# Graph attention and nucleus diffusion: rank constants formed at the start, and half of a block of S products moved from ahead of the first attention into it

## The chip, the cores and the metric

The kernel runs on one core of a Trainium2 chip. A core has five engines that work side by side, each through its own queue in order: TensorE (PE in the profile; PEld is its weight load), VectorE (DVE), ScalarE (ACT), GpSimd (POOL) and SyncE (SP, which issues most of the loads and stores). The metric is the time of one execution in microseconds on the device. Before the change the median of four runs is 3581.87 us (3580.59 to 3583.27).

## The reference

There are 2708 nodes with 512 features, in two layers; each adds its result to its input, `x = x + f(relu(layernorm(x)))`.

Layer 0 is graph attention with 8 heads over an adjacency matrix `adj` of zeros and ones. Layer 1, cut to what matters here:

```python
S = adj + eye(n)
Rf = S / row sums of S              # forward, rows scaled
Rb = S / column sums of S           # as written, scaled over its rows
Xf, Xb, Xa = X, X, X
for s in range(2):
    logits = (Xa @ W1) @ W2 @ (Xa @ W3).T
    A = softmax over the nucleus of each row   # largest entries up to 0.9 of the mass
    Xf = Rf @ Xf;  Xb = Rb @ Xb;  Xa = A @ Xa
    Z = Z + Xf @ U1[s] + Xb @ U2[s] + Xa @ U3[s]
out = layernorm(X + Z) * gamma + beta
```

Ties at the edge of the nucleus are broken by the index of the column; the kernel needs ranks of equal keys for that in its second step.

## The kernel before

All of it is in one function. The nodes are cut into 22 tiles of 128 rows (`NT`; the last has 20), the tiles into 11 `pairs`, and every two pairs into a `quad` of four tiles (`quads`).

**Layer 0** (lines 203 to 460) is put in order by a scheduler from the dependences of its instructions. It begins with LayerNorm, one tile at a time (`moments` and `cleared`, from lines 133 and 219 on): VectorE's statistics, POOL's power, VectorE's `h`, POOL's maximum with zero, then PE's transposes (L268) and products (L277, L280), and VectorE's `fw` (L298). Its pool of large tiles (`fw`, `b_b`, `beta_b` and others) is freed at the end. Its last tiles are normed at about 1060 us, and VectorE's first and last splits of `v` follow at 1070 and 1081 us.

**Constants.** Behind layer 0 stand the small constants of layer 1, and with them those for the ranks, lines 498 to 506: `ones` filled with 1, `across` its running sum along the row, `down` the same number down the partitions (by way of the identity matrix), and `below_d`, which is 1 where `across < down`. `ones` and `across` lie in a pool `ramps` of their own, which is freed at once.

**Layer 1** takes two steps, `s` = 0 and 1 in the code. Step 1 of the title is the first, `s = 0`, where `last` is false; the change is in it alone. PE, ACT, DVE and SP run in the order in which the code is written (`manual_schedule`); POOL is put in order by the scheduler. For each pair there is a `Logits` object `lg[i]`:

- `queries()` loads its `q_t` (L525, on SP). `products()` forms its two rows of logits (L538 on PE) and copies them into two tiles `p` (L540 on ACT). There are four `p` tiles, so pair i takes those of pair i - 2. Its products go through the tiles `t`, two in PSUM, which the transposes of the attention use too.
- `maxima` (L565, DVE) and `exp()` (L575 to L597): two exponentials over each row on ACT, some points on POOL, and then for all pairs but the first twelve passes on ACT that the code calls looks (L572 with `nth`), and POOL's sums of them.
- `search()` on VectorE finds the threshold of the nucleus: rounds that measure the mass above a point (L651), into which `early()` puts the maxima of the pair after the next, then `late()`, and then `finish()` (L845, L847, L780), which writes the kept rows into two tiles `keep` and ends in a branch (L929) for the rare rows with ties; `rden` (L940) is the first instruction behind it.
- `attended()` turns the rows of `keep` (L1098 on PE, L1102 on ACT) and multiplies them by the values `va` (L1120), in 12 steps of up to four tiles of columns; `mixed()` then multiplies by `U3` (L1160, two batches) and projects the new keys (L161).

Beside this run the products with `S`, quad by quad, each in two parts. `part(half, b)` returns a list of small steps, and `paced(steps, n)` runs the first n of them and takes them off the list. In the first step of the diffusion, for even b, it is 22 steps `product(c)`: each loads `hl` (512 KB) and `s_r` (256 KB) over SP (L1003, L1005) and does eight matmuls (L1013) into four tiles `q`. For odd b it is 11 steps: `across` (L1020, four ACT copies and stores `tt_d`), four `through` with U1 (eight matmul records each, L1030, with a load `u_k` on SP), `scaled` (L1040, four ACT copies `xe`), four `through` with U2, and `scaled`. The first `scaled` of an odd part has its rows split at once by VectorE (`split_rows`, L182 and L183) and stored by POOL (L184, to `fhl_d`); those of the second wait in `pending`.

Ahead of the first attention the code runs parts 0 and 1 and then, while VectorE searches for the first pair, all of part 2:

```python
                    others = part(half, 2)
                    paced(others, len(others))
                done = []
                ...
                for g in range(-1, NP):
                    fills = []
                    if last or g >= 0:
                        others = part(half, g + 2 if last else g + 3)
                    if 0 <= g < NP - 2:
                        lg[g + 2].products()
```

So the loop at g = 0 takes the third pair's products, then the attention of the first pair with part 3 as `others`: one step of them behind each of the 12 steps of `attended`, two at the start of `mixed` and one at each of its eight products. At the same time VectorE searches for the second pair. g = 1 takes the fourth pair's products, the attention of the second pair and part 4, and so on.

Of the kernel before, what the change touches and what calls it, by code (L numbers as in the profile page):

```python
# [9 lines left out]
F32 = mybir.dt.float32  # L10
BF16 = mybir.dt.bfloat16
# [4 lines left out]
OP = mybir.AluOpType  # L16
# [8 lines left out]
P = 128  # L25
# [28 lines left out]
def kernel(  # L54
# [19 lines left out]
    nc = tc.nc  # L74
# [6 lines left out]
    NT = -(-N // P)  # L81
# [14 lines left out]
    const = ctx.enter_context(tc.tile_pool(name="const", bufs=1))  # L96
# [21 lines left out]

    ident = const.tile([P, P], F32, name="ident")
    make_identity(nc, ident)  # L120
    nhalf = const.tile([P, 1], F32, name="nhalf")
    nc.vector.memset(nhalf, -0.5)

# [79 lines left out]
    with ExitStack() as l0:  # L203
# [13 lines left out]
        with tc.tile_pool(name="l0w", bufs=1) as wp, tc.tile_pool(name="l0p", bufs=2) as pp, \  # L217
# [44 lines left out]
            for t in range(NT):  # L262
# [8 lines left out]
                for k in range(KD):  # L271
                    nc.scalar.activation(h_t[:, k, :pr], pt[:, k, :pr], AF.Copy,
                                         accum_out=hs[:, k, t:t + 1])
# [138 lines left out]
        for ci, tiles in enumerate(tchunks):  # L412
# [4 lines left out]
            for t in range(NT):  # L417
# [5 lines left out]
                if pr < P or cw < wide:  # L423
                    nc.gpsimd.memset(s_c.bitcast(F32), 0.0)
                nc.scalar.activation(s_c[:pr, :cw], a_c[t][:pr, :cw], AF.Copy,  # L425
                                     accum_out=cpart[:pr, t, ci:ci + 1])
# [67 lines left out]
    for i in range(G + 1):  # L494
        nc.vector.memset(weights[:, i:i + 1], float(1 << i))
    NA = len(ABOUT)

    down = const.tile([P, 1], F32, name="down")
    below_d = const.tile([P, P], BF16, name="below_d")
    with tc.tile_pool(name="ramps", bufs=1) as pool:  # L500
        ones = pool.tile([P, P], F32, name="ones")
        across = pool.tile([P, P], F32, name="across")
        nc.vector.memset(ones, 1.0)
        nc.vector.tensor_tensor_scan(across, ones, ones, 0.0, OP.add, OP.bypass)
        nc.vector.scalar_tensor_tensor(ones, across, 1.0, ident, op0=OP.mult, op1=OP.mult, accum_out=down)
        nc.vector.tensor_scalar(below_d, across, down, None, op0=OP.is_lt)

    class Logits:

# [440 lines left out]
    for s in range(STEPS):  # L950
        last = s == STEPS - 1
        with ExitStack() as st:
# [129 lines left out]
            def paced(steps, n):  # L1082
                for step in steps[:n]:
                    step()
                del steps[:n]
# [151 lines left out]
            with tc.manual_schedule(engines={PE, ACT, DVE, SP}):  # L1237
                junk = wide.tile([P, -(-N // 4) * 2], F32, name="junk", bufs=1)
                lg = [Logits(pools, s, grp, keys, rank) for grp in pairs[:2]]
                half = []  # L1240
                others = part(half, 0)
                if last:
                    lg[0].queries()
                    lg[0].products()
                    for load in values(nc.gpsimd):
                        load()
                    heads, counts = ranked(junk.bitcast(BF16)[:, :N], list(range(early_tiles, NT)), "keep", 2)
                    steps = lg[0].exp(looks=False)
                    paced(heads, len(heads))
                    for step in lg[0].maxima + steps + counts:  # L1250
                        step()
                    lg[1].queries()
                    paced(others, NT // 2)
                    spread()
                    lg[1].products()
                    paced(others, len(others))
                else:
                    paced(others, 3)
                    for n, (t, v) in enumerate(unasked):
                        asked(s, slice(n * early_tiles // len(unasked) * P, (n + 1) * early_tiles // len(unasked) * P))  # L1260
                        paced(others, 1)
                        split_rows(parts, nc.vector, v[:rows[t]], t, vhl_d)
                        v_t = transposed(up, ps_t, v, rows[t], "v_t")
                        project(small, ps_t.tile([P, 512], F32, name="t"), v_t, t, s)
                    asked(s, slice(early_tiles * P, N), nc.gpsimd)
                    lg[0].queries()
                    lg[1].queries()
                    ahead = [c for c in chunks if c[1] <= early_tiles * P]
                    lg[0].products(ahead)
                    paced(others, 3)  # L1270
                    lg[0].products(chunks[len(ahead):])
                    steps = lg[0].exp(looks=False)
                    for step in lg[0].maxima + steps:
                        step()
                    paced(others, 9)
                    lg[1].products()
                    paced(others, len(others))
                    others = part(half, 1)
                    loads = values(nc.sync)
                    while others:  # L1280
                        paced(others, 1)
                        paced(loads, 2)
                    others = part(half, 2)
                    paced(others, len(others))
                done = []
                ready = None
                left = []
                for g in range(-1, NP):

                    fills = []  # L1290

                    if last or g >= 0:
                        others = part(half, g + 2 if last else g + 3)
                    if 0 <= g < NP - 2:
                        lg[g + 2].products()
                    if g < 0:
                        paced(left, len(left))
                    if g + 3 < NP:
                        lg.append(Logits(pools, s, pairs[g + 3], keys, rank))
                        lg[g + 3].queries()  # L1300
                    norms = [normed(t, y) for t, y in done] if last else []
                    done = []

                    if g == NP - 1 and not last:
                        asked(s + 1, slice(0, early_tiles * P))
                        heads, counts = ranked(junk.bitcast(BF16)[:, :N], list(range(early_tiles)), "p", 4)
                        fills += heads + [lambda: paced(counts, len(counts))]
                    if g >= 0:
                        final = g == NP - 1 and not last
                        att = attended(pairs[g], *ready, fills, others, 1 if final else 3 if g or not last else len(tgroups) + 1)  # L1310
                    def early(g=g):
                        if g + 2 < NP:
                            fills.extend(lg[g + 2].exp())
                        first, *more = lg[g + 2].maxima if g + 2 < NP else [lambda: None]

                        def begin():
                            if g >= 0:
                                paced(pending, len(pending))
                            first()

                        return begin, lambda: [x() for x in more], lambda: [rest() for rest in norms]

                    def late(g=g):
                        if g >= 0:
                            out_ = rest_of(att)
                            if last:
                                done.extend(zip(pairs[g], out_))
                            else:
                                mixed(pairs[g], out_, others, fills, final)
                            keeps = min(len(others), len(quads[g // 2 + 1])) if last and others else 0  # L1330
                            while len(others) > keeps or fills:
                                paced(others, min(2, len(others) - keeps))
                                paced(fills, 1)
                            left.extend(others)
                            others.clear()
                            return


                        paced(fills, len(fills))
                        if last:  # L1340
                            paced(others, len(others))

                    if g + 1 < NP:
                        opened = None
                        if g >= 0:
                            opened = Opened(lg[g + 1], True, junk)
                            opened.bracket()
                        ready = search(lg[g + 1], opened, junk, early, late)
                        if g < 0 and not last:
                            paced(pending, len(pending))  # L1350
                    else:
                        for rest in norms:
                            rest()
                        paced(pending, len(pending))
                        late()
                if last:
                    for rest in [normed(t, y) for t, y in done]:
                        rest()
                    paced(stores, len(stores))
# [31 lines left out]
```

## Time and profile before

| | |
|---|---|
| median of 4 runs | 3581.87 us |
| the profiled execution | 3589.24 us, its span 3587.4 us |
| PE busy | 3329.9 us, 93% |
| DVE busy | 2655.7 us, 74% |
| ACT busy | 1504.2 us, 42% |
| POOL busy | 859.4 us, 24% |
| mean granted PE clock | 0.974 |
| part 2 of S, products L1013 | 1172.0 to 1239.1 us |
| first L1098 of the first attention | 1246.87 us |
| first L1098 of the second attention | 1348.52 us |

In the rows below a line of the timeline begins with its start, its duration, engine, source line and operation, then `out<-in` by the program's names, the shape and how many instructions follow one another; in brackets stands how long the engine was idle before, and what released it. For PE a matmul of four-byte values shows as more than one record. A row of windows has the stretch, its length, the busy time of PE, PEld, DVE, ACT and POOL with their instructions, the granted PE clock as a share of full speed, the mean busy share of the 16 DMA engines, and GB/s.

### The profile page before, as it was taken

How to read it: one execution, taken by the hardware profiler on the slowest of the kernel's cores; microseconds unless marked ns; L12 is line 12 of the kernel's file. 1: busy time of each engine (PE TensorE's matmuls, PEld its weight loads, DVE VectorE, ACT ScalarE, POOL GpSimd, SP SyncE). 2: the span in 40 equal slices, each digit the busy share in tenths (PEclk: the TensorE clock that was granted, in tenths of full speed). 3: DMA queues.
4: the chain of work that ended last, by engine and by line, in shares of the span. 5: the costliest groups of instructions: out<-in, count | busy, mean ns of one | idle time of the engine just before them, and what ended most of it. 6: DMA issues, size and time to landing. Idle time of an engine off the chain costs nothing. (4 is left out here: it accounts for less than half of the span.)

```text
span 3587.4 us, 34134 instructions
## 1 busy us (share of the span) xinstructions
PE 3329.9 (93%) x10797; PEld 1721.2 (48%) x10797; DVE 2655.7 (74%) x4828; ACT 1504.2 (42%) x2269; POOL 859.4 (24%) x1074
## 2 busy tenths in 40 slices
PE   7998999998978799999999999889999999999877
PEld 4433333333445546455464544355555555565433
DVE  4587888889985645463754655598889998889994
ACT  2344211111103666564656672344545564445610
POOL 4114241415321111222121221311112222122211
PEclk9999999999999999999999999999999999999989
DMA  3477424232318726344452622684556545566433
GB/s 115 145 246 247 153 95 138 76 123 85 102 67 292 270 91 208 103 164 162 152 195 90 214 82 69 206 286 144 197 182 232 173 166 183 197 208 205 157 129 119
DMA packets 251348, 579.99 MB, mean 162 GB/s; under 512 B 33945, under 2 KB 67593, under 8 KB 248291
## 3 DMA queue, kind: packets, MB, share of 16 engines
q1 hardware_dynamic: 229063, 503.39, 42.3%
q0 software_dynamic: 22064, 74.09, 5.3%
q8 instruction: 86, 1.41, 0.2%
q14 instruction: 135, 1.11, 0.1%
HBM read 471.68 MB, written 105.68 MB: 161 GB/s over the span
## 5 line engine op out<-in xcount | busy, mean ns | idle before, releaser
L1120 PE MATMUL a<-va,at 128*128 128x512 f32 (+2 forms) x1936 | 889.0, 599 | 7.4 <-ACT at L1102 7.3
L443 PE MATMUL po<-e,fw 128*65 128x512 f32 (+4 forms) x2112 | 838.5, 552 | 33.3 <-DVE e L441 21.0
L441 DVE SCALAR_TENSOR_TENSOR e<-r_b,kk,a_c 128x512 f32<-128x512 f32 (+4 forms) x1056 | 750.4, 739 | 72.2 <-PE po L443 21.8
L572 ACT ACTIVATE junk_a<-p,nth 128x2708 uint8<-128x2708 f32 (+1 forms) x240 | 612.7, 2553 | 57.2 <-POOL nth L587 52.7
L1010 PE MATMUL q<-hl,s_r 128*128 128x512 f32 x1936 | 528.5, 422 | 66.4 <-DMA s_r<-s_d 62.5
L443 PEld LDWEIGHTS po<-e,fw 128*65 128x65 f32 (+1 forms) x2112 | 286.7, 140 | 545.3 <-issue 270.4
L1120 PEld LDWEIGHTS a<-va,at 128*128 128x128 f32 (+2 forms) x1936 | 338.8, 187 | 378.1 <-issue 335.5
L1010 PEld LDWEIGHTS q<-hl,s_r 128*128 128x128 f32 x1936 | 364.6, 192 | 219.1 <-issue 63.1
L651 DVE SCALAR_TENSOR_TENSOR junk<-p,th 128x2708 bf16<-128x2708 f32 (+1 forms) x132 | 424.9, 3219 | 3.2
L1102 ACT COPY at<-t 128x512 f32<-128x512 f32 (+3 forms) x308 | 140.1, 476 | 495.4 <-PE t L1098 491.5
L1013 PE MATMUL q<-s_r,hl 128*128 128x512 f32 (+1 forms) x1056 | 282.9, 415 | 40.4 <-DMA s_r<-s_d 37.5
L1030 PE MATMUL q<-u_k,v 128*128 128x512 f32 x704 | 317.0, 593 | 0.8 <-ACT v L1020 0.8
L540 ACT COPY p<-t 128x452 f32<-128x452 f32 (+2 forms) x264 | 129.9, 537 | 341.0 <-PE t L538 268.4
L1013 PEld LDWEIGHTS q<-s_r,hl 128*128 128x128 f32 x1056 | 193.2, 195 | 124.1 <-issue 49.6
L565 DVE TENSOR_REDUCE nmx<-p 128x1 f32<-128x2708 f32 (+1 forms) x44 | 130.5, 2968 | 110.3 <-ACT p L540 110.3
L1030 PEld LDWEIGHTS q<-u_k,v 128*128 128x128 f32 x704 | 133.6, 190 | 150.5 <-issue 145.0
L847 DVE MAX8 vn<-keep 128x8 f32<-128x2708 f32 (+1 forms) x66 | 196.8, 2982 | 2.3
L425 ACT ACTIVATE s_c<-a_c 128x512 fp32r<-128x512 f32 (+3 forms) x132 | 76.2, 577 | 248.5 <-DMA a_c<-in_adj_t_dram 122.8
L1160 PE MATMUL a<-u_k,v_t 128*128 128x512 f32 (+1 forms) x352 | 170.0, 623 | 1.9 <-DMA u_k<-in_L_gnn_U_dram 1.9
L1098 PEld LDWEIGHTS t<-ident,keep 128*128 128x128 f32 (+1 forms) x968 | 114.9, 140 | 114.2 <-issue 89.4
L538 PE MATMUL t<-keys,q_t 128*128 128x452 f32 x528 | 149.1, 403 | 21.8 <-ACT p L540 21.4
L1098 PE MATMUL t<-ident,keep 128*128 128x128 f32 (+1 forms) x968 | 147.3, 275 | 18.9 <-DVEq L934 11.6
(311 smaller groups left out, 3311.8 us busy)
## 6 DMA issues: line engine op xcount, KB each, us to landing
s_r<-s_d SPq DMA_DIRECT2D x330, 256.0 KB
hl<-vhl_d SPq DMA_DIRECT2D x132, 512.0 KB
hl<-fhl_d SPq DMA_DIRECT2D x132, 512.0 KB
hl<-bhl_d SPq DMA_DIRECT2D x132, 512.0 KB
u_k<-in_L_gnn_U_dram SPq DMA_DIRECT2D x184, 256.0 KB
arow<-in_adj_dram SPq DMA_DIRECT2D x21, 1354.0 KB
s_d<-s_c SPq DMA_DIRECT2D x88, 256.0 KB
a_c<-in_adj_t_dram SPq DMA_DIRECT2D x84, 256.0 KB
```

The source lines that it names most:

```text
L441: nc.vector.scalar_tensor_tensor(e[:pr, :cw], r_b[:pr, i, :cw], kk[:pr, t, hd:hd + 1], a_c[t][:pr, :cw], op0=OP.max, op1=OP.mult)
L443: nc.tensor.matmul(po[i][:, :cw], lhsT=fw[:pr, t, hd, :], rhs=e[:pr, :cw], start=(t == 0), stop=(t == NT - 1))
L538: nc.tensor.matmul(pl[:, :c1 - c0], lhsT=q[:, i], rhs=self.keys[:, c0:c1], start=(i == 0), stop=(i == 1))
L572: nc.scalar.activation(junk[:pr], self.p[i][:pr], func, **kw)
L651: nc.vector.scalar_tensor_tensor(self.junk_b[:pr], p, th, p, op0=OP.is_ge, op1=OP.mult, accum_out=dst)
L847: v.max(vs, keep[0][:pr])
L1010: nc.tensor.matmul(half[j], lhsT=s_r[:, j * P:(j + 1) * P], rhs=hl[:, h], start=(c == 0 and h == 0), stop=(c == NT - 1 and h == 1))
L1013: nc.tensor.matmul(half[j][:, :w], lhsT=hl[:, h, j * P:(j + 1) * P], rhs=s_r[:, :w], start=(c == 0 and h == 0), stop=(c == NT - 1 and h == 1))
L1030: nc.tensor.matmul(half[j], lhsT=across_t[-1][k][:, j * P:(j + 1) * P], rhs=u_k, start=(start and k == 0), stop=(start and k == KD - 1))
L1098: nc.tensor.transpose(pt[:rows[c], j, :pr], keep[i][:pr, cols[c]], ident[:pr, :pr])
L1120: nc.tensor.matmul(pa[:pr], lhsT=at[:rows[c], j, :pr], rhs=va[:rows[c], c, :], start=(c == 0), stop=(c == NT - 1))
L1160: nc.tensor.matmul(pz[i][:rows[t]], lhsT=v_t[i][:, k, :rows[t]], rhs=u_k, start=(k == 0), stop=(k == KD - 1))
```

## The change

It has two edits. The constants for the ranks are formed right behind the identity matrix, ahead of layer 0, and their pool `ramps` is freed before the pool of layer 0 is opened. And of part 2 only 11 of the 22 products run ahead of the first attention (`NT // 2`); the other 11 stay in `others`, and part 3 is put behind them, so that the first attention has 22 steps instead of 11 beside it. Later attentions have no rest to take over. In the last step of the diffusion nothing changes.

```diff
     make_identity(nc, ident)
+    down = const.tile([P, 1], F32, name="down")
+    below_d = const.tile([P, P], BF16, name="below_d")
+    with tc.tile_pool(name="ramps", bufs=1) as pool:
+        ones = pool.tile([P, P], F32, name="ones")
+        across = pool.tile([P, P], F32, name="across")
+        nc.vector.memset(ones, 1.0)
+        nc.vector.tensor_tensor_scan(across, ones, ones, 0.0, OP.add, OP.bypass)
+        nc.vector.scalar_tensor_tensor(ones, across, 1.0, ident, op0=OP.mult, op1=OP.mult, accum_out=down)
+        nc.vector.tensor_scalar(below_d, across, down, None, op0=OP.is_lt)
...
     NA = len(ABOUT)
-
-    down = const.tile([P, 1], F32, name="down")
-    below_d = const.tile([P, P], BF16, name="below_d")
-    with tc.tile_pool(name="ramps", bufs=1) as pool:
...
                         paced(loads, 2)
                     others = part(half, 2)
-                    paced(others, len(others))
+                    paced(others, NT // 2)
...
-                    if last or g >= 0:
-                        others = part(half, g + 2 if last else g + 3)
+                    if last:
+                        others = part(half, g + 2)
+                    elif g >= 0:
+                        others += part(half, g + 3)
```

In the order of the instructions the first edit moves the loads `b_b` and `beta_b` on SP from the head of the queue to between the two loads `v_b`, since `b_b` lies where `ones` and `across` were, and VectorE's and POOL's statistics of some of layer 0's first tiles ahead of a product `fw`. The second moves on PE, ACT, SP and POOL what belongs to the steps named; the order on VectorE in layer 1 stays the same.

More of the change, by code (lines that the diff above doesn't have):

```diff
@@ L496 @@
     NA = len(ABOUT)
-    down = const.tile([P, 1], F32, name="down")
-    below_d = const.tile([P, P], BF16, name="below_d")
-    with tc.tile_pool(name="ramps", bufs=1) as pool:
[L501 to L506, printed above, removed]
     class Logits:
```

## The prediction

> **What bounds the kernel now.** I read the page first: PE is busy for 93% of the span, and from the start of the diffusion step to 2000 us for 97% of it (483.4 of 500 us in the windows from 1500 to 2000). Whatever lengthens PE's chain there lengthens the kernel. Then I read the timeline of each engine around the moved half block. PE:
>
> ```profile
> 1192.75 2.11 PE L1013 MATMUL q<-s_r,hl 128*128 128x512 f32 x8 [0.70 <-DMA s_r<-s_d]
> 1196.93 7.31 PE L1013 MATMUL q<-s_r,hl 128*128 128x512 f32 x24 [2.07 <-DMA s_r<-s_d]
> ...
> 1239.13 0.98 PE L538 MATMUL t<-keys,q_t 128*128 128x452 f32 x4
> ...
> 1246.87 1.09 PE L1098 MATMUL t<-ident,keep 128*128 128x128 f32 x8 [0.20 <-ACT p L540]
> ...
> 1321.72 1.12 PE L148 MATMUL t<-ident,xa 128*128 128x128 f32 x4 [3.09 <-ACT xa L1128]
> 1322.63 9.59 PE L1160 MATMUL a<-u_k,v_t 128*128 128x512 f32 x16
> 1332.05 1.95 PE L161 MATMUL t<-v_t,kw 128*128 128x128 f32 x16
> 1333.83 7.03 PE L1160 MATMUL a<-u_k,v_t 128*128 128x512 f32 x16
> 1340.30 1.39 PE L538 MATMUL t<-keys,q_t 128*128 128x452 f32 x4
> ```
>
> Eight records are one product. Nine end by 1194.8 and three follow from 1196.93, so the eleventh ends near 1201.5. The other eleven last until L538 at 1239.13, with waits for their loads between them: two windows show the cause, a DMA share of 0.95 in the second.
>
> ```profile
> 1172.00:1201.50 29.50, 23.99 (x87) 18.07 (x86) 22.21 (x48) 22.63 (x21) 8.65 (x11) 0.88 0.77 261
> 1201.50:1239.10 37.60, 25.97 (x92) 18.73 (x92) 16.63 (x46) 21.03 (x16) 3.81 (x9) 0.91 0.95 343
> ```
>
> ScalarE and VectorE in the same stretch, and at the end of the first attention:
>
> ```profile
> 1222.57 0.19 ACT L572 ACTIVATION_READ_ACCUMULATOR junk_a<-p,nth 128x1 f32 x1
> 1239.75 0.97 ACT L540 COPY p<-t 128x452 f32<-128x452 f32 x2 [16.99 <-PE t L538]
> ```
>
> ```profile
> 1282.59 0.43 DVE L182 TENSOR_SCALAR split_hl<-xe 128x512 int32<-128x512 int32 x1 [25.59 <-ACT xe L1040]
> 1291.52 3.03 DVE L845 SCALAR_TENSOR_TENSOR keep<-p,th 128x2708 f32<-128x2708 f32 x1
> 1313.32 3.04 DVE L780 SCALAR_TENSOR_TENSOR keep<-p,cut 128x2708 f32<-128x2708 f32 x1 [4.45 <-PE t L1098]
> 1323.55 0.17 DVE L940 RECIPROCAL rden<-den 128x2 f32<-128x2 f32 x1 [3.43 <-DVEq L929]
> ```
>
> Two things stand here. ACT's looks at the second pair end at 1222.76, so ACT is 17 us ahead of PE, not more. And VectorE's `finish()` of the second search stands behind four splits of `xe`, which wait for U1's products on PE. It ends at 1323.55, 16.75 us before PE comes to the fourth pair's L538 at 1340.30. That L538's results go into the `p` tiles of the second pair, which `finish()` reads to its end: the built program lets the first copy L540 into each `p` tile wait for VectorE as well as PE.
>
> **Edit 2, the start of the first attention.** Eleven products go from PE's path ahead of the attention, 1201.5 to 1239.1, 37.6 us; each took its loads (256 and 512 KB) along on SP, which now issues the third pair's eight `q_t` loads behind product eleven; they have 20 us. But the order of ACT is unchanged there: twelve looks, then the copies L540. They cannot start before 1222.8. From the first copy to the first L1098 took 1246.87 - 1239.75 = 7.1 us, so the attention starts at 1229.9 at the earliest. Only 17 of the 37.6 us come off; PE stands idle for some 20.
>
> Idle costs clock too:
>
> ```profile
> 1322.00:1324.00 2.00, 2.00 (x6) 1.28 (x6) 0.17 (x1) 1.13 (x2) 0.00 (x0) 0.50 0.00 0
> ```
>
> After the wait of 3.09 us the granted clock was 0.50, and the first L1160 batch took 9.59 instead of 7.03 us, 2.6 lost. In L538 PE shares the pace with ACT's copies, so I take 2 us (bounds 0 and 2.6). Start: 1232, 15 us earlier.
>
> The Trainium skill ("TensorE: Matmul & The Clock Gate", Part 1) says that the clock halves after an idle window of about 3.4 us and needs about as long at work to come back, and so speaks against a change that opens gaps. This trace differs a little, as 3.09 us sufficed. By the page a gap would cost an estimated 1.7 us, in place of my 2.
>
> **Edit 2, inside the attention.** In the first attention a step took 7.31 us (1259.04 to 1266.35) with a U product of 3.43 in it, so 3.87 bare; in the second attention a step with a product took 5.72. A product there costs 1.85 us, eleven cost 20.4. What gives its place is U: the attention's twelve steps now take the eleven products and `across`, and the eight U products and two `scaled` go into `mixed`. The second attention before is the model for the new first one: from L1098 at 1348.52 to its last L1120 at 1413.19, 64.7 us with eleven products. So it ends at 1232 + 64.7 = 1296.7 (before: 1318.6).
>
> `mixed` took 1318.63 to 1340.30 = 21.7 us, of which 15.9 are work (transposes 0.44, two L1160 batches of 6.84 at full clock, L161 1.78) and 5.8 idle and half clock. With two U products ahead of the transposes that gap closes. Eight times 3.43 come in: 15.9 + 27.4 = 43.3, to 1340.0. PE alone would come out even with before (1340.3).
>
> What moves along on the other queues: U's eight `u_k` loads share three buffers with the U3 loads of `mixed`. L1160 waited for `u_k` 8.1 us in 12 waits, 0.7 each; mostly a product of 3.43 stands between two loads, so 0, at most eight such waits, 5.4. `across` (four ACT copies of 0.5, and 2.2 us of stores on POOL) falls into the twelfth step, behind the looks and ahead of U. The `fhl_d` stores move on POOL in front of the sums after the looks (L595 to L597) and the keys' splits; VectorE asks for those sums only after `finish()`.
>
> **Edit 2, VectorE behind it.** The queue order on VectorE stays: the four splits of `xe` ahead of `finish()`. Their input now comes with the fourth U1 product, which ends 6.86 + 0.44 + 1.71 + 3.43 + 1.71 + 3.43 = 17.6 us into `mixed`, 1314.3 (before: 1280.7). ACT's copy and the first split follow 1 us later, 1315.3. Splits took 8.9 us here and 7.9 in the third attention (1493.06 to 1500.94); `finish()` took 32.0 with a wait of 4.45 for PE that is gone, 27.6. Its end, and the release of `p`: 1315.3 + 8.4 + 27.6 = 1351.3, where it was 1323.55. PE is there at 1340.0 and stands for some 11 us. The slack of 16.75 us that covered this wait has become its size: 28 us later on VectorE, none on PE. From 1351.3 on, 7.1 us of copies and 2 of half clock: the second attention starts at 1360.4, 11.9 us later than 1348.52.
>
> Behind that nothing gives it back: VectorE waits for PE in the second attention anyway (15.90 us at L780), and everything after is chained to PE. The maxima for the fourth pair come some 5 us too late for ACT's place for them; as ACT runs a step ahead I take 0 for that (bounds 0 and 4). Edit 2: +12; bounds -3 (VectorE in time) and +18 (these 4 and some of the waits for `u_k`).
>
> **Edit 1.** The four VectorE instructions of the ramps (0.17 + 0.42 + 0.37 + 0.29 us from 1068.23) leave a gap in which VectorE would wait for POOL:
>
> ```profile
> 1069.22 0.29 DVE L506 TENSOR_SCALAR below_d<-across,down 128x128 bf16<-128x128 f32 x1
> 1070.02 0.53 DVE L390 TENSOR_SCALAR o<-o,ln_mv,ln_rs 20x512 f32<-20x512 f32 x1 [0.51 <-POOL ln_rs L141]
> ```
>
> So 0 there. At the start they cost VectorE 0.7 us in waits for POOL, but `b_b` now lies where `ones` and `across` were: its load waits for them, and queued behind it on SP are `beta_b`, the second `v_b` and `w1`. The first PE work waits for `w1` (16.10): up to 0.9 us later. On the other side the scheduler moves LayerNorm's statistics of the next tiles ahead of the first `fw` product on VectorE, which bears on a wait that PE pays:
>
> ```profile
> 33.75 0.82 PE L268 MATMUL tp<-ident,h 128*128 128x128 f32 x4 [1.57 <-POOL h L226]
> 34.36 5.17 PE L277 MATMUL pf<-w_sb,h_t 128*128 128x512 f32 x8
> ```
>
> 1.57 idle and 1.5 of half clock (5.17 against 3.70 later) can go, less 0.9: I take -2, bounds -3 and +1.
>
> **Sum.** The profiled execution took 3589.24 us (span 3587.4): +12 - 2 = +10 makes it 3599. The median of the runs is 3581.87, 7.4 lower; the same +10 makes 3592. A measurement tells about 0.2%, 7.2 us, from no change.
>
> **Rivals.** *ACT alone limits.* If VectorE's `finish()` is through before PE comes (U's products sooner, or `p` let go earlier), PE stands at 1340.0 against 1340.3 and only half clock and the start count: -2 to +0, 3580 to 3582: no change. The point is 1340: `finish()` must end 11 us sooner than I have it. For it: the splits may be quicker by the 5 us that they wait for stores. Against: its parts are measured on rows that recur in four attentions within 1 us. Chance 0.22. *The gain is real.* If the looks end near 1201.5 and VectorE keeps up, 37.6 + 5.8 - 20.4 = 23 us go: 3557 with edit 1. Against it stands ACT's row at 1222.57, whose chain the change does not touch. Chance 0.06. *More is lost.* ACT's late maxima hold back the transposed tiles in the second attention and the half clock reaches into L1120: +18, 3598. It belongs to my side; chance 0.12. The forecast has 0.60, its own range 3586 to 3598. That edit 1 does nothing at all is worth 2 us and decides nothing.
>
> **Numbers.** Slower by over 0.2% (above 3589) is the forecast save its lower edge and the last rival, 0.54 + 0.12 = 0.66; within 0.2% is the first rival with that edge, less 0.01 for its own lower end, 0.27; faster is the second rival and that end, 0.07. The range 3579 to 3601 takes in the first rival and the upper bounds and leaves out 0.2.
>
> **What would show it.** Right: L540 for the third pair starts at 1223 with PE idle some 20 us ahead of it; the first L1098 at 1230 to 1232; L182 on `xe` near 1315 after a wait of about 60 us; L940 near 1351; the fourth pair's L540 idle for 11 us, released by VectorE; the second attention from 1358 to 1362 (each less 2 by edit 1); from there on the distance to before constant. Wrong: L940 ahead of PE's L538, looks that end well before 1222, or a distance that shrinks again after 1400.

## The result, and the profile after

The changed kernel takes 3589.91 us (median of 42 runs) where the kernel before takes 3582.84 us (64 runs): a ratio of 1.002, with a 95% interval from 1.0014 to 1.0025, 5 to 9 us slower. The profiled execution took 3595.43 us, its span 3593.6 us (before: 3589.24 and 3587.4).

The timeline of PE in the changed kernel, around the moved half block (start, duration, engine, line, operation, tiles, shape, and in brackets the idle time before and what ended it):

```profile
1200.20 0.99 PE L538 MATMUL t<-keys,q_t 128*128 128x452 f32 x4
1220.62 6.75 PE L538 MATMUL t<-keys,q_t 128*128 128x452 f32 x16 [19.42 <-ACT p L540]
...
1228.90 1.09 PE L1098 MATMUL t<-ident,keep 128*128 128x128 f32 x8 [0.19 <-ACT p L540]
...
1337.37 1.38 PE L538 MATMUL t<-keys,q_t 128*128 128x452 f32 x4
1349.20 7.51 PE L538 MATMUL t<-keys,q_t 128*128 128x452 f32 x20 [10.45 <-ACT p L540]
1356.80 1.20 PE L1098 MATMUL t<-ident,keep 128*128 128x128 f32 x8
```

Two long waits are new. The first stands where the eleven products were taken away: PE comes to the third pair's logits at 1200.20, and ACT's first copy comes only at 1220. The second stands ahead of the fourth pair's logits. ACT's rows say what ended each:

```profile
1217.50 2.55 ACT L572 ACTIVATE junk_a<-p,nth 128x2708 uint8<-128x2708 f32 x1
...
1220.05 0.95 ACT L540 COPY p<-t 128x452 f32<-128x452 f32 x2
...
1348.61 0.97 ACT L540 COPY p<-t 128x452 f32<-128x452 f32 x2 [10.05 <-DVEq L929]
```

At 1220.05 nothing is in brackets: ACT was at work, with the last of its twelve looks. At 1348.61 it waited, and DVEq L929 is VectorE's queue at the branch that ends `finish()`. VectorE ahead of it:

```profile
1309.65 0.43 DVE L192 TENSOR_SCALAR split_hl<-xe 128x512 int32<-128x512 int32 x1 [61.22 <-ACT xe L1040]
...
1318.39 3.03 DVE L845 SCALAR_TENSOR_TENSOR keep<-p,th 128x2708 f32<-128x2708 f32 x1
...
1338.88 1.09 DVE L900 SCALAR_TENSOR_TENSOR short<-fr,den 128x2 int32<-128x2 f32 x1
...
1340.48 1.68 DVE L905 TENSOR_TENSOR fr<-fr,thr 128x2 f32<-128x2 f32 x1
...
1344.90 0.14 DVE L926 TENSOR_SCALAR code_i<-code 1x1 int32<-1x1 f32 x1
1348.61 0.17 DVE L940 RECIPROCAL rden<-den 128x2 f32<-128x2 f32 x1 [3.57 <-DVEq L929]
```

It sat for 61 us on the first `xe` (L192 is L182 of before), split, ran `finish()`, and let the `p` tiles go 11 us after PE was there.

From first L1098 to first L1098 the change adds up so. The first attention starts 17.97 us earlier (1246.87 to 1228.90). From there to the fourth pair's L538 PE needs 108.47 us instead of 93.43, 15.04 more, for the eleven products that are now inside (the U products were inside before as well). From that L538 to the second attention it needs 19.43 us instead of 8.22, 11.21 more. The sum is +8.3 us at the second attention.

### The profile page after: what moved, and what is told of

Its sections match the earlier page's. It is cut to its first block, busy times and chain, and to the rows that moved or that the text cites. A ratio compares the mean times of both kernels' runs of the same rounds, so it can differ in the third digit from the quotient of the medians.

```text
span 3593.6 us, 34143 instructions
## 1 busy us (share of the span) xinstructions
PE 3333.6 (93%) x10797; PEld 1721.5 (48%) x10797; DVE 2656.2 (74%) x4828; ACT 1505.2 (42%) x2269; POOL 866.2 (24%) x1074
## 5 line engine op out<-in xcount | busy, mean ns | idle before, releaser
L453 PE MATMUL po<-e,fw 128*65 128x512 f32 (+4 forms) x2112 | 847.6, 557 | 28.1 <-DVE e L451 20.3
L453 PEld LDWEIGHTS po<-e,fw 128*65 128x65 f32 (+1 forms) x2112 | 288.2, 140 | 547.9 <-issue 275.1
L1102 ACT COPY at<-t 128x512 f32<-128x512 f32 (+3 forms) x308 | 140.1, 476 | 495.8 <-PE t L1098 491.8
L540 ACT COPY p<-t 128x452 f32<-128x452 f32 (+2 forms) x264 | 130.7, 537 | 342.3 <-PE t L538 331.7
L565 DVE TENSOR_REDUCE nmx<-p 128x1 f32<-128x2708 f32 (+1 forms) x44 | 130.5, 2968 | 107.1 <-ACT p L540 107.1
L538 PE MATMUL t<-keys,q_t 128*128 128x452 f32 x528 | 155.1, 418 | 54.2 <-ACT p L540 49.4
L1098 PEld LDWEIGHTS t<-ident,keep 128*128 128x128 f32 (+1 forms) x968 | 115.2, 140 | 114.2 <-issue 88.1
L1098 PE MATMUL t<-ident,keep 128*128 128x128 f32 (+1 forms) x968 | 147.5, 275 | 21.8 <-DVEq L934 14.4
```

The lines of the kernel that those rows point to most:

```text
L453: nc.tensor.matmul(po[i][:, :cw], lhsT=fw[:pr, t, hd, :], rhs=e[:pr, :cw], start=(t == 0), stop=(t == NT - 1))
L538: nc.tensor.matmul(pl[:, :c1 - c0], lhsT=q[:, i], rhs=self.keys[:, c0:c1], start=(i == 0), stop=(i == 1))
L1098: nc.tensor.transpose(pt[:rows[c], j, :pr], keep[i][:pr, cols[c]], ident[:pr, :pr])
```

## The experiments

The theory going in: ACT's looks hold the first attention, and `finish()` behind the splits of `xe` holds the second. The rival: the moved products cost as much inside as ahead, and VectorE and ACT only fill PE's waits. Time differences come from the ratios; one profile stands beside each.

**Each edit alone.** The first run keeps the constants at the front and puts `paced(others, len(others))` back; the second is the kernel before with the second edit.

> Only the first edit: the constants for the ranks ahead of layer 0, all 22 products of part 2 ahead of the first attention as before. Theory (the order of layer 0's start costs PE one wait of 1.57 us and some half clock, which go): -2 us, a ratio of 0.9994, with the second attention some 2 us earlier than before's 1348.5. Rival (layer 0 is chained to other waits and takes the 2 us back): the second attention at 1348.5, ratio 1.0000.

> Only the second edit: half of part 2 inside the first attention, the rank constants where they were. Theory (the released p tiles come late, PE stands for some 10 us ahead of the second attention): +9 to +12 us, ratio 1.0025 to 1.0033; PE's L538 for the fourth pair waits 10 us or more for ACT's copy, which waits for VectorE. If the two edits disturb each other, this run less 2 us is not the changed kernel.

The first edit alone: ratio 0.9994 (0.9981 to 1.0007), second attention at 1342.37. The size is as expected, but the interval holds no change as well. In its profile the second attention stands 6.2 us earlier than before's and not 2: PE, which waits for loads in part 2, came to the third pair's L538 at 1234.60 instead of 1239.13. The second alone: 1.0040 (1.0024 to 1.0055), more than the 1.0025 to 1.0033 expected, though the interval covers these; second attention at 1365.38, PE's wait 10.33 us. The mechanism belongs to the second edit. With the second edit in both, this profile and the changed kernel's differ by 8.6 us at the second attention (1365.38 and 1356.80), since ACT's looks ended at 1228.85 here and at 1220.05 there: a single profile places a stage no closer than that. The two together would give +12 us where the changed kernel has +7; the intervals cover that gap, and a disturbance between the edits is not shown.

**How many stay ahead.**

```diff
-                    paced(others, NT // 2)
+                    paced(others, 17)
```

> The changed kernel with 17 of the 22 products ahead of the first attention instead of 11. Theory (VectorE's splits of xe and finish() behind them are the delay; they follow the place of U1 in the order): PE has work until ACT's looks end near 1220, so the idle time ahead of L540 for the third pair is under 2 us; xe comes near 1290 to 1295 and the first instruction behind finish() near 1327, when PE gets there too; the second attention starts at about 1334 instead of 1356.8 (before: 1348.5): 15 us faster than before, ratio 0.9958 (bounds 0.9950 and 0.9975). Rival (a product costs as much inside the attention as ahead of it, VectorE being beside the point): only the idle time ahead of the first attention changes hands, second attention at 1346 to 1349, ratio 0.9994 to 1.0000.

Ratio 0.9982 (0.9972 to 0.9992), second attention at 1337.41: faster than before, short of the 0.9958. PE's idle time ahead of the first attention went as expected, so PE came to the fourth pair at 1319.09, not 1327. VectorE was 2 us later than expected, and the wait stayed:

```profile
1287.93 0.43 DVE L192 TENSOR_SCALAR split_hl<-xe 128x512 int32<-128x512 int32 x1 [41.55 <-ACT xe L1040]
...
1318.12 3.97 DVE L921 COPY flag<-flag_t 1x3 f32<-1x3 f32 x4
...
1329.06 0.17 DVE L940 RECIPROCAL rden<-den 128x2 f32<-128x2 f32 x1 [6.41 <-DVEq L929]
```

The first split came 2 us sooner than the 1290 to 1295 expected for `xe`. `finish()` took 34.3 us this time (1294.81 to 1329.06): L921 3.97 us where it took 0.67 before, and the branch 6.41 where it took 3.43. The last section says what stands beside L921. PE stood for 9.19 us.

**finish() ahead of the splits.** The splits of part 3's first `xe` stay in `pending`, and the second `scaled` is held until after `mixed`.

```diff
-            for u, inv, to, now, name in ((u1[1], rinv, fhl_d, b > 1, "xe"),
+            for u, inv, to, now, name in ((u1[1], rinv, fhl_d, b > 1 and b != 3, "xe"),
...
+                        paced(held, len(held))
                         others += part(half, g + 3)
+                        if g == 0:
+                            held.append(others.pop())
```

> The changed kernel, but VectorE runs finish() of the second pair's search ahead of the four splits of part 3's first xe (the splits stay behind it; the second scaled of part 3 is put behind mixed so that the xe tiles suffice). PE's order is the same. Theory (the splits ahead of finish() hold the p tiles): the first instruction behind finish() comes before 1310 instead of 1348.6, PE's L538 for the fourth pair no longer waits for VectorE at 1337 to 1339, and the second attention starts at 1345 to 1346, 11 us earlier than in the changed kernel; whole kernel 3 to 4 us faster than before, ratio 0.9990. Rival (ACT's copies or the loads are late by themselves): the second attention stays at 1353 to 1357, ratio 1.0010 to 1.0020.

Ratio 0.9985 (0.9973 to 0.9996), second attention at 1346.03, both close to what was expected.

```profile
1250.46 3.04 DVE L845 SCALAR_TENSOR_TENSOR keep<-p,th 128x2708 f32<-128x2708 f32 x1 [4.30 <-PE t L1098]
...
1294.30 0.17 DVE L940 RECIPROCAL rden<-den 128x2 f32<-128x2 f32 x1 [3.82 <-DVEq L929]
```

PE's order is that of the changed kernel; VectorE's order, and the place of four ACT copies, differ. The 10.45 us are gone; the 2.60 that remain are those copies (L1040, 2.42 us from 1335.72), which this edit itself put ahead of L540. So the second wait is the place of `finish()` behind the splits. The next run puts that right: `finish()` becomes part of the step that holds the second `scaled` (`others[-1] = lambda: (finish(), end())` at g = 0), PE's and ACT's orders stay, and 17 products are ahead.

> 17 products ahead, and finish() of the second pair's search ahead of the four splits of part 3's first xe, now without moving the second scaled: PE's and ACT's orders are those of 17 ahead. Theory (with 17 ahead the only loss left is PE's 9.2 us ahead of the second attention, and it comes from finish() behind the splits): no wait at L538 for the fourth pair, PE there at 1319 and the second attention at 1327 to 1329; 10 us faster than 17 ahead alone, ratio 0.9955 (bounds 0.9945 and 0.9968). Rival (something else holds the p tiles or PE loses the time later): ratio 0.9975 to 0.9985 as with 17 ahead.

Ratio 0.9958 (0.9944 to 0.9973). The loads let PE through some 8 us later than in the other profile with 17 ahead (L538 for the third pair at 1222.55 against 1213.89), and so the second attention stands at 1335.16; but there is no wait ahead of it:

```profile
1326.95 1.39 PE L538 MATMUL t<-keys,q_t 128*128 128x452 f32 x4
1328.63 1.12 PE L538 MATMUL t<-keys,q_t 128*128 128x452 f32 x4 [0.29 <-ACT p L540]
```

**No looks for the second pair.** VectorE measures the three points instead.

```diff
-                            fills.extend(lg[g + 2].exp())
+                            fills.extend(lg[g + 2].exp(looks=last or g >= 0))
...
-                        if g >= 0:
+                        if g >= (0 if last else 1):
                             opened = Opened(lg[g + 1], True, junk)
```

> The changed kernel, but for the second pair ACT takes no looks; VectorE measures the three points itself at the start of its search (six instructions of 3.04 us in its 61 us of idle time). Theory (ACT's looks until 1220 hold the first attention): L540 for the third pair starts when PE comes, near 1200 (up to 1203 if the first search's branch is late), first L1098 at 1207 to 1211 instead of 1228.9; the rest follows 18 to 22 us earlier with PE's wait of about 10 us for finish() as it is: xe at 1288 to 1292, second attention at 1335 to 1339; 10 to 13 us faster than before, ratio 0.9964 to 0.9972. Rival (ACT only fills PE's wait; loads or the p tiles hold the start): first L1098 later than 1222, ratio 1.0000 to 1.0020.

> Control: the looks of the second pair on VectorE as in e5_no_looks, but all 22 products ahead of the first attention (the first edit is in). Theory: PE comes to L540 at 1235 with ACT long free either way and VectorE is done with its rounds before xe comes at 1278, so nothing changes against the first edit alone: ratio 0.9994, second attention near 1342 to 1346. Rival (the looks cost time by themselves, wherever the products stand): faster by 5 us or more than the first edit alone.

> 11 products ahead as in the changed kernel, no looks on ACT for the second pair, and finish() ahead of the splits: both waits of the changed kernel taken away at once. Theory (the two waits, 20 us and 10 us, were the whole of what the moved half block lost): first attention from 1207 to 1211, PE at the fourth pair's L538 near 1316 to 1320 without a wait, second attention at 1324 to 1328, 20 to 25 us ahead of before; ratio 0.9930 to 0.9945. Rival (what is gained ahead of 1330 is given back behind, as VectorE and ACT are late for the third and fourth pair): second attention at 1328 or earlier but ratio 0.9960 or more.

The control with 22 ahead came out as expected, 0.9992 (0.9979 to 1.0005), second attention at 1342.38. With 11 ahead the first L1098 stood at 1208.34 instead of 1228.90: the looks do hold it, and the first half of the theory stands. But the ratio was 1.0064 (1.0039 to 1.0090), and with `finish()` ahead of the splits besides 1.0027 (1.0013 to 1.0041). Both expectations were wrong by some 30 us. PE and ACT without looks, in that order:

```profile
1259.09 4.08 PE L1120 MATMUL a<-va,at 128*128 128x512 f32 x4 [20.79 <-ACT at L1102]
```

```profile
1253.27 0.20 ACT L575 ACTIVATE nmx<-nmx 128x1 f32<-128x1 f32 x1 [25.52 <-DVE nmx L565]
```

ACT's place for the third pair's exponential came 20 us earlier (behind the fourth L1102; in the changed kernel L575 stood there at 1248.22 without a wait), and VectorE's maxima for it, behind six more measurements, 15.4 us later (L565 at 1250.27 and 1260.19 instead of 1234.82 and 1244.74). ACT stood, and the attention's copies L1102 stood behind it. I had counted VectorE's 18 us against its idle time at the end of the search, and not against who waits in the middle. The repair is to form these maxima ahead of the measurements (L565 behind the splits, by calling `early()` at the start of that search):

```diff
             o = Opened(lg, False, junk)
+            for step in early() if grp[0] == 2 and s == 0 else []:
+                step()
             for j in range(NA):
...
-            if it == 1:
+            if it == 1 and not (begins and grp[0] == 2 and s == 0):
                 afterwards.extend(early())
```

> As e8_both_waits_gone, and VectorE forms the third pair's maxima ahead of its six measurements instead of inside the rounds behind them. Theory (what e5 and e8 lost is one new wait: ACT stands at L575 for 25 us on maxima that VectorE's 18 us of measurements push back, and the attention's copies L1102 stand behind it): L575 waits under 2 us, PE's 20 to 27 us of idle time inside the first attention are gone, the fourth pair's L538 comes at 1316 to 1320 without a wait, second attention at 1323 to 1328; ratio 0.9930 to 0.9950. Rival (VectorE is now the bound of the stretch: its 18 us more come out again as a wait for finish() or later maxima): second attention at 1335 or later, or a ratio above 0.9965.

> As e9_maxima_first with 8 products ahead instead of 11. Theory (PE then comes to L538 for the third pair near 1190, but the p tiles are those of the first pair, which its finish() lets go at 1194 to 1197, and the three products cost some 2 us each inside): first L1098 at 1202 to 1205, second attention within 3 us of e9_maxima_first, ratio within 0.0010 of it. Rival (every product that is moved saves 1.5 us or more, with no bound yet): 0.0015 faster or more.

With 11 ahead: 3560.36 us, ratio 0.9940 (0.9920 to 0.9960), the lowest of all, though its interval overlaps the next two in the table below. Lines from 714 on count two higher here (L1100 is L1098, L931 is L929):

```profile
1200.76 1.09 PE L1100 MATMUL t<-ident,keep 128*128 128x128 f32 x8 [0.19 <-ACT p L540]
...
1314.00 1.38 PE L538 MATMUL t<-keys,q_t 128*128 128x452 f32 x4
1315.68 1.11 PE L538 MATMUL t<-keys,q_t 128*128 128x452 f32 x4 [0.30 <-ACT p L540]
...
1322.22 1.09 PE L1100 MATMUL t<-ident,keep 128*128 128x128 f32 x8 [0.20 <-ACT p L540]
```

ACT's L575 came at 1220.10 without a wait. With both waits and the new one gone, the moved half block does bring its time. The three orders were not run together with all 22 products ahead. The looks alone gave nothing there (0.9992), and before's PE has no wait for `finish()` that could be won; so I put the gain down to the move, by argument and not by a run. With 8 ahead, the second attention was at 1321.89, no earlier, since the third pair's copies now waited for the first pair's `finish()`:

```profile
1191.55 0.97 ACT L540 COPY p<-t 128x452 f32<-128x452 f32 x2 [15.27 <-DVEq L931]
```

Its ratio is 0.9959 (0.9939 to 0.9978): no gain from three more products. The point lies 0.0019 above that with 11 ahead, outside the 0.0010 expected; whether it is a loss the overlapping intervals leave open.

**Two terms of finish().** One run leaves out POOL's two additions `y + va` behind the first attention, the other the flags and the branch for the second pair.

```diff
-                        if n == 0:
+                        if n == 0 and (last or grp[0]):
                             nc.gpsimd.tensor_tensor(y[:pr], y[:pr], va[:pr, t, :], op=OP.add)
```

```diff
         def branch():
+            if s == 0 and grp[0] == 2:
+                return
```

> The changed kernel without POOL's two additions of va to y (L1169, 128x512) behind the first pair's attention; that sum is left out of the result. Theory (finish() measured 30.2 us instead of my 27.6 because VectorE's small instructions there stand until POOL's additions end): the tail of finish() from the last L780 to L926 takes 3.6 to 3.8 us instead of 6.1, with no L900 or L905 over 0.3 us, and PE's wait at the fourth pair's L538 is 2 to 2.5 us shorter (about 8). Rival (the stretch comes from something else, such as the 2.5 us of DMA issue): the tail still takes 5 us or more.

> The changed kernel without the end of finish() for the second pair: no flags and no branch for rows with ties (that repair is left out for this pair). Theory (the p tiles are let go at the branch, 9.8 us behind the last reading of them that always happens, at 1338.8): L538 for the fourth pair waits under 2 us instead of 10.5, the second attention starts at 1346 to 1348; 9 to 11 us faster than the changed kernel, ratio to before 0.9985 to 0.9995. Rival (the release comes with VectorE's next instruction wherever the branch is, or ACT is late by itself): the wait stays at 8 us or more, ratio 1.0015 or more.

Without the additions the tail took 3.65 us (L897 at 1332.24 to L926 at 1335.89; 6.09 in the changed kernel), and PE's wait fell from 10.45 to 8.38 us, as expected. This is from one run.

Without the branch the wait went as expected, and the second attention started at 1342.11, 14.7 us earlier than in the changed kernel; but the ratio was 1.0021 (1.0007 to 1.0035), as slow as it. The gain was lost again. Part of it is seen in the second attention:

```profile
1381.81 5.63 PE L1122 MATMUL a<-va,at 128*128 128x512 f32 x8 [5.36 <-ACT at L1104]
```

ACT waited there for the fourth pair's maxima (4.32 and 4.05 us at L575), which VectorE forms behind `finish()` and the rest of its work; the third attention was 116.3 us behind the second, where it was 109.3 in the changed kernel. PE's wait of 10 us had also been the time in which VectorE caught up. That explains 7.1 of the 14.7 us. At 2073 the profile still was 6.2 us ahead of the changed kernel's; what is lost behind that, in the loads ahead of the last step, I can't name, and this profiled execution (3604.7 us) lies 11 us above the median of its own runs (3594.06), where before's lies 6 above.

**All of them side by side**, by where the second attention starts (us). "Maxima first" has the looks on VectorE and `finish()` ahead of the splits as well; the run without the additions has one execution and so no ratio:

| | second attention | span | span less start | ratio |
|---|---|---|---|---|
| 8 ahead, maxima first | 1321.89 | 3564.3 | 2242.4 | 0.9959 |
| 11 ahead, maxima first | 1322.22 | 3557.5 | 2235.3 | 0.9940 |
| 17 ahead, finish first | 1335.16 | 3576.7 | 2241.5 | 0.9958 |
| 17 ahead | 1337.41 | 3571.0 | 2233.6 | 0.9982 |
| first edit alone | 1342.37 | 3579.3 | 2236.9 | 0.9994 |
| 22 ahead, no looks | 1342.38 | 3581.8 | 2239.4 | 0.9992 |
| finish first | 1346.03 | 3578.6 | 2232.6 | 0.9985 |
| no additions | 1348.37 | 3581.8 | 2233.4 | - |
| before | 1348.52 | 3587.4 | 2238.9 | 1 |
| changed kernel | 1356.80 | 3593.6 | 2236.8 | 1.0020 |
| both waits gone | 1358.61 | 3597.1 | 2238.5 | 1.0027 |
| no looks | 1365.14 | 3609.0 | 2243.9 | 1.0064 |
| second edit alone | 1365.38 | 3597.3 | 2231.9 | 1.0040 |
| no branch | 1342.11 | 3602.8 | 2260.7 | 1.0021 |

Save for the last row the rest of the kernel takes 2238 us, 6 more or less, wherever the second attention starts. To within that scatter, what is won or lost ahead of it stays.

## Why the prediction was right

The forecast was 3592.0 us, 10 more than before; it is 7 more, in the range, and by the mechanism that it named. Step by step, each forecast less the 2 us of the first edit, against the changed kernel's profile:

- *Start of the first attention* by ACT's looks, L540 at 1221 and L1098 at 1230: measured 1220.05 and 1228.90. The low clock behind 19.42 us of idle (granted 0.54 from 1220.62 to 1227.40) cost 1.5 us (6.75 for four products, 5.24 at the pace of 1.31), not 2. That the looks are the cause is shown: without them L1098 came at 1208.34. That they ended within 1 us of the forecast is luck: in the five profiles with 11 ahead and looks the first L540 behind them comes from 1214.39 to 1228.85.
- *The attention* to 1294.7: 1293.5. *PE at the fourth pair* at 1338.0: 1337.37.
- *The split of xe* at 1313.3: 1309.65, 3.7 us sooner. One is the attention's end. The rest is a mis-sized step: I let `xe` wait for the whole fourth U1 product, but its first tile needs only the first quarter of it, 2.6 us earlier.
- *Splits* 8.4: 8.74. *finish()* 27.6: 30.2. The term missed POOL: two small instructions of the tail stood until POOL's additions ended, 2.5 us. I had taken it from an attention in which POOL was silent there.
- *Its end* at 1349.3: 1348.61, as by luck the early split (3.7 us sooner) and the longer splits and `finish()` (2.9 us) nearly cancel. *The wait* 11: 10.45. The low clock behind it cost 1.0 us (7.51 for five products, 6.55 at the pace of 1.31), where 2 were forecast. *Second attention* at 1358.4, 9.9 behind before: 1356.80, 8.3.
- *The fourth pair's late maxima* at 0, bounds 0 and 4: from second to third attention 109.26 us against 108.82, so 0.4. The run without the branch shows how near that was: with PE sooner the same maxima cost 7.5.
- *The first edit* at -2: 2.45 us at the first product with `fw` (L453 at 138.78, L443 before at 141.23), and 0.9994 by itself. The load `w1` did not come later (first PE work at 15.91, before at 16.10), so the 0.9 that I had set against the gain did not come at that load.
- *Nothing gives it back*: the distance to before is 8.3, 8.7, 8.7, 8.7, 10.2, 10.2, 9.1 and 9.4 us at the second to ninth attention. In the profiled pair 6.5 of it go between 2079 and 2456, ahead of the last step, where PE waits for loads of `s_r`; but that stretch takes 375 to 383 us over the kernels here (389.6 without the branch), with 376.2 in the changed kernel and 382.6 in before near its two ends. The forecast had named a distance that shrinks after 1400 as a sign against it. I read it as scatter, and the table fits that; it is not shown.

The rivals: *ACT alone limits* is what the run with `finish()` ahead of the splits became: its second attention stands 2.5 us ahead of before's, where 0 to -2 were worked out. That run's 0.9985 is 5 us. *The gain is real* (23 us and 2 for the first edit) was measured at 0.9940, 21 us, but holds only with looks, splits and maxima all out of the way. *More is lost* did not come: the waits for `u_k` stayed away.

## What to carry to other kernels

Work that is taken out of the way of the bounding engine brings only the part up to the next engine that is due, so follow each engine's queue to the moment when it would be late, and in the middle of its work too, not only at its end. A buffer may be let go only at the end of a whole sequence in its reader's queue (here behind the branch, 9.8 us after the last L780), and an instruction whose input is moved later takes everything queued behind it along (here ACT's copies behind L575). Where a move loses time, look for the order behind it before giving it up: the same half block with three orders changed was 0.6% faster than before instead of 0.2% slower.

## What the runs showed of the hardware

**VectorE and POOL stop each other.** In the changed kernel POOL's additions stand beside the tail of `finish()`:

```profile
1337.79 2.17 POOL L1169 TENSOR_TENSOR yo<-yo,va 128x512 f32<-128x512 f32 x1 [8.69 <-ACT yo L1167]
...
1340.85 1.28 POOL L1169 TENSOR_TENSOR yo<-yo,va 128x512 f32<-128x512 f32 x1
```

They end at 1339.96 and 1342.13; L900 and L905 of VectorE, 0.16 us each elsewhere, end at 1339.97 and 1342.16. Without the additions both took 0.16 us. In that same run POOL's L183, a split of the keys (`kq_hl`), took 3.21 us (1318.34 to 1321.55) where the one before took 0.46, beside VectorE's L845 (1318.21 to 1321.23). The Trainium skill ("SBUF — State Buffer", Who interferes with whom) says that a VectorE instruction with two inputs in SBUF and a GpSimd instruction that reads SBUF exclude each other, and that the second waits until the first has ended. Both cases here agree that one stands until the other ends. Which came first is plain for L900 and L183; the record of L905 begins 0.37 us ahead of POOL's second addition, so there it is not shown.

The run with 17 ahead gives the same picture for VectorE copies with one input: of the four L921, 0.17 us each elsewhere, the first took 1.29 us and the last 2.05. They end at 1319.41 and 1322.09; POOL's L183 and L1169 beside them end at 1319.39 and 1322.05. That is the 3.3 us by which L921 was longer there.

**The branch behind finish() varies.** VectorE stood at L929 for 3.43 to 6.41 us at the second pair in the profiles shown, and 20 such waits come to 82.2 us in before. The forecast had taken the parts of `finish()` to recur within 1 us; in before this wait alone was 5.43 us at the first pair and 3.43 at the second. What makes the difference was not tried.
